# Rows that are put off, counted for four tiles at once: a top-p attention step on one Trainium2 core

## The chip, the cores and the metric

The kernel runs on one core of one Trainium2 chip. The metric is the device time of one execution in microseconds; the median of several executions is compared. A core has five engines, each with its own queue of instructions that it works off in order: TensorE (PE, with its weight loads PEld), VectorE (DVE), ScalarE (ACT), GpSimd (POOL) and SyncE (SP, which only issues DMAs here). They wait for each other, and for DMAs, through semaphores.

## The reference

Four layers of a graph network on 4096 nodes with 256 features and one 4096x4096 adjacency matrix. The layer that matters here is the second one, which runs two steps of this:

```python
def _top_p_attention(X, W1, W2, W3):
    q = X @ W1.T @ W2.T
    k = X @ W3.T
    logits = q @ k.T / TAU
    probs = jax.nn.softmax(logits, axis=-1)
    idx = jnp.argsort(-probs, axis=-1)
    sp = jnp.take_along_axis(probs, idx, axis=-1)
    cs = jnp.cumsum(sp, axis=-1)
    keep_sorted = cs - sp < TOP_P            # TOP_P = 0.9
    ...
    A = probs * mask
    return A / jnp.maximum(A.sum(-1, keepdims=True), 1e-12)

for n in range(STEPS):                       # STEPS = 2
    A = _top_p_attention(Xa, W1, W2, W3)
    Xf = R @ Xf
    Xa = A @ Xa
    Z = Z + Xf @ U1[n].T + Xa @ U2[n].T
```

R is the adjacency matrix with the identity added, rows normalised. The sum X + Z is layer-normalised, then the layer's residual is added and normalised again: two normalisations per row, each with one reciprocal square root.

## The kernel before

The 4096 rows are worked on as NT = 32 tiles of 128 rows (P = 128), the 4096 columns as NLC = 8 chunks of 512. In the profile, layer 0 lies at 0 to about 390 us, step 0 of the attention layer from there to about 1440 us, step 1 from about 1440 to 2690 us, the last two layers after that.

An iteration i of `run_step` has three tiles in work: logits of tile i + 2 (matmuls L414, copied by ACT), the selection for tile i + 1, and the mixing product of tile i (`acc_bank`, L761 and L769). The selection finds the threshold of each row from the largest entries: maxima by groups of eight (`cand`, L433), a scan of their sum, a threshold `t_thr`, then `match_replace` (L658) and four passes over the row of exponentials (L663). Rows for which this way is not sure to give the exact set are marked in a column `bad` (L564), 1.0 or 0.0 for each of the 128 rows. They are put off: their numbers go into a list in DRAM, `list_d`, and jobs (`put_off`, L897 and on) later take 128 of them at a time, compute them by an exact way and write them over the first result. Step 0 has one such job, step 1 has three (`LATER = (1, 3)`).

The list is made by `flag` (L582 to L607), once per tile. With `bad` as the moving operand PE multiplies by a matrix of ones (the tile's count, in every partition) and by a triangular matrix `before` (how many bad rows stand ahead of this one in the tile), L592 and L593; in the profile each is two passes. Three DVE operations follow: the new running count `sofar` (L595), `slot` (L599) and `slots` (L600), which is the place in the list for a bad row, and a spare place for all others. Then POOL scatters the tile's 128 row numbers to these places by an indirect DMA (L606). It is 64 scatters in all, each to the tensor `list_d` of its step. The scatters of a step have each to wait until the one before has landed, since they write one tensor.

The products of `flag`, of the queries (L394) and of the mixing (L822) take turns in the two halves of one PSUM bank, `mm_bank`.

An iteration's operations are hung on the eight chunks g = 0 to 7 in a fixed order:

```python
at(2, tops, cd, rounds)
at(2, pick, cd, rounds)
at(4, flag, cd)
```

`at(5, settle)` follows in step 1, where `match_replace` and L663 are. In step 0 the indirect gathers of the kept neighbours (`G`, L672, 512 in all) are hung on g = 4 to 7 and fill POOL's queue. A scheduler then orders instructions by priority for each engine, within what the program's dependences allow; each engine executes its own list in that order.

At the end of an iteration `after` makes the output of tile i: `mix` (h, L822 and L824) and two layer normalisations, whose reciprocal square roots are single operations on POOL (`rstd`, L199). DVE uses them at L848 (first normalisation, with the residual) and L204 (second).

A job starts at the end of the iterations that `starts` names: i = 30 in step 0 and i = 9, 20 and 30 in step 1. It starts with a DMA of 128 entries of the list on SP's queue (`to_l`, L888), a DVE operation on them (`from_l`, L890) and an indirect gather of the rows on POOL (`xf_new`, L812); its other stages run beside the next eight iterations. A job may start only when the scatters of all tiles up to i + 1 have been made.

Of the kernel before, what the change touches and what calls it, by code (L numbers as in the profile page):

```python
# [11 lines left out]
F32 = mybir.dt.float32  # L12
# [7 lines left out]
ALU = mybir.AluOpType  # L20
# [4 lines left out]
P = 128  # L25
# [15 lines left out]
LATER = (1, 3)  # L41
ROUNDS = 9
NG_LATER = 18
KEPT = 16
MATCHES_LATER = 3
MATCHES = 1
# [10 lines left out]
def gnn_stack(ctx, tc, x, adjt, adjn, w0, b0, w1, w2t, w3t, u1t, u2t, ln_g, ln_b, w2, b2, w3, b3, out):  # L57
# [3 lines left out]
    nc = tc.nc  # L61
    N = x.shape[0]
    NT = N // P
    LC = min(512, N)
    NLC = N // LC
# [20 lines left out]
    def half(bank):  # L86
        turns[bank] ^= 1
        return (mm_bank if bank == "mm" else acc_bank)[:, turns[bank], :]
# [268 lines left out]
    with tc.tile_pool(name="l1", bufs=1, reuse_waits="tile") as l1:  # L357
# [64 lines left out]
        def small(tag, w=1, dt=F32, bufs=2):  # L422
            if cur["late"]:
                return cur["lw"].tile([P, w], dt, tag=tag, name=f"{tag}_l", bufs=2 if w == 1 else 1)
            return work.tile([P, w], dt, tag=tag, name=tag, bufs=bufs)
# [108 lines left out]
        def pick(st, rounds):  # L534

            top, thr, base = st["top"], st["thr"], st["base"]
            W = 8 * rounds  # L540
            cs = small("cs", W + 1, bufs=1)
            if base is None:
                nc.vector.memset(cs[:, 0:1], 0.0)
                te = small("te", W + 1)
                nc.scalar.activation(te, top, AF.Exp, bias=st["m"], scale=1.0)
            else:
                nc.vector.tensor_copy(cs[:, 0:1], base)
                te = top
            nc.vector.memset(cs[:, W:], 3e38)
            nc.vector.tensor_tensor_scan(cs[:, 1:W], te[:, : W - 1], te[:, : W - 1], cs[:, 0:1], op0=ALU.add, op1=ALU.max)  # L550
            under, part = small("under", W, bufs=1), small("part", W, bufs=1)
            count = small("count")
            nc.vector.tensor_scalar(under, cs[:, :W], thr, 0.0, op0=ALU.is_lt, op1=ALU.add, accum_out=count)
            nc.vector.scalar_tensor_tensor(part, cs[:, 1:], thr, under, op0=ALU.is_ge, op1=ALU.mult)
            st["t"] = t = small("t_thr")
            nc.vector.scalar_tensor_tensor(part, part, 1.0, te[:, :W], op0=ALU.mult, op1=ALU.mult, accum_out=t)
            st["left"] = left = small("left")
            nc.vector.tensor_scalar(part, te[:, :W], t, 0.0, op0=ALU.is_ge, op1=ALU.add, accum_out=left)
            nc.vector.tensor_sub(left, left, count)
            st["bad"] = bad = small("bad")  # L560
            nc.vector.tensor_tensor(bad, te[:, W - 1 : W], te[:, W:], op=ALU.max)
            nc.vector.tensor_tensor(bad, bad, t, op=ALU.is_ge)
            most = 0.0 if sparse(st) else 8.0 * (MATCHES if base is None else MATCHES_LATER)
            nc.vector.scalar_tensor_tensor(bad, left, most, bad, op0=ALU.is_gt, op1=ALU.max)  # L564
            if sparse(st):

                same = small("same")
                for r in range(8, W, 8):
                    nc.vector.tensor_tensor(same, top[:, r - 1 : r], top[:, r : r + 1], op=ALU.is_equal)
                    nc.vector.tensor_tensor(bad, bad, same, op=ALU.max)  # L570
                st["w"] = w = small("w", W)
                kept = small("kept")
                nc.vector.scalar_tensor_tensor(w, te[:, :W], t, te[:, :W], op0=ALU.is_ge, op1=ALU.mult, accum_out=kept)
                whole(st, kept)
# [7 lines left out]
        def flag(st):  # L582


            pb = half("mm")
            later = st.get("later")
            if later is None:
                nc.tensor.matmul(pb[:1, 0:1], st["bad"], ones_col, start=True, stop=True)
                st["nb"] = small("nbad", 1, I32)[:1, :]
                nc.scalar.copy(st["nb"], pb[:1, :1])  # L590
                return
            nc.tensor.matmul(pb[:, 0:1], ones_sq, st["bad"], start=True, stop=True)  # L592
            nc.tensor.matmul(pb[:, 1:2], before, st["bad"], start=True, stop=True)  # L593
            sofar, slot = small("sofar"), small("slot")
            nc.vector.tensor_add(sofar, later["base"], pb[:, 0:1])  # L595

            i = st["tile"]
            at, rows_i = slots_of[cur["n"]][:, i : i + 1], ids[:, i : i + 1]
            nc.vector.scalar_tensor_tensor(slot, pb[:, 1:2], later["base"], spare, op0=ALU.add, op1=ALU.subtract)  # L599
            nc.vector.scalar_tensor_tensor(at, slot, st["bad"], spare, op0=ALU.mult, op1=ALU.add)  # L600
            later["base"] = sofar
            if i == NT - 1 and cur["n"] == 0:

                st["to"] = to = small("to_last", 1, I32, 1)
                nc.vector.scalar_tensor_tensor(to, st["bad"], float(P), rows_i, op0=ALU.mult, op1=ALU.add)
            nc.gpsimd.indirect_dma_start(  # L606
                out=list_d[cur["n"]], out_offset=bass.IndirectOffsetOnAxis(ap=at, axis=0), in_=rows_i, in_offset=None)  # L607

        def bit_by_bit(st):

# [333 lines left out]
        def run_step(n, es):  # L944

            later = {"base": spare0}
            tiles = {}
            last = []  # L950
            jobs = []
# [26 lines left out]
                cur["late"] = False  # L978
                return [[f] for f in after(n, job["st"])]

            starts = {min((k + 1) * NT // LATER[n] - 1, NT - 2): k for k in range(LATER[n])}
            for i in range(-2, NT):
                st = tiles.pop(i, None)
                cd = tiles.get(i + 1)
                nxt = None
                if i + 2 < NT:

                    nxt = {"tile": i + 2, "q": cur["qs"].pop(0), "e": logits_in(es[i % 2]), "later": later, "G": {}}
                    tiles[i + 2] = nxt
                if i + 1 == NT and n == 0:  # L990
                    for fs in last:
                        for f in fs:
                            f()
                    last = []
                    left_over(n, es[NT % 2], later)
                ops = {}

                def at(g, f, *args):
                    ops.setdefault(g, []).append(lambda: f(*args))

                for g, fs in zip((1, 2), last):
                    for f in fs:
                        at(g, f)
                if 0 < i + 2 < NT - 1:
                    turned = []
                    g = 1 if n else 6
                    at(g - 1, lambda i, turned: turned.append(transposed(cur["xa"][:, i + 3, :])), i, turned)
                    at(g, lambda turned: cur["qs"].append(query(None, turned[0])), turned)
                if cd is not None:
                    peak_groups(cd, NG_LATER if n else ngr)  # L1010
                    at(1, exp_rows, cd)
                for job in jobs:
                    at(1, advance, job)
                if cd is not None:
                    rounds = ROUNDS if n else KEPT // 8
                    at(2, tops, cd, rounds)
                    at(2, pick, cd, rounds)
                    at(4, flag, cd)
                    if n == 0:
                        for k in range(8):  # L1020
                            at(4 + k // 2, gather, cd, k)
                    else:
                        at(5, lambda cd: [None for _ in settle(cd)], cd)
                for job in jobs:
                    if n and i + 1 == NT:
                        at(4, advance, job)
                    at(6, advance, job)
                if i + 1 == NT and n == 0:
                    cur["next"] = load_halves(es[1 - NT % 2], xf_d, nc.sync)
                if i < 0:  # L1030
                    now = FIRST[n][i + 2]
                else:
                    now = [i + 2] if FIRST[n][1][-1] < i + 2 < NT else []
                pieces(n, st, nxt, ops, now)
                last = [[f] for f in after(n, st)] if st is not None else []
                if i in starts:
                    k = starts[i]
                    if len(jobs) > (i == NT - 2):
                        last = finish(jobs.pop(0), last)
                    e = es[NT % 2] if k + 1 == LATER[n] else es[2]  # L1040
                    jobs.append({"stages": put_off(n, k, e, later)})
                    if i < NT - 2:
                        advance(jobs[-1])
# [185 lines left out]
```

## Time and profile before

| | us |
|---|---|
| median of 3 runs | 3159.19 (3156.39 to 3160.6) |
| the profiled execution | 3226.1 |
| its span in the trace | 3224.4 |
| PE busy | 2945.7 (91%) |
| DVE busy | 2260.9 (70%) |
| ACT busy | 1729.6 (54%) |
| POOL busy | 778.7 (24%) |
| scatter L606, one, on POOL | 1.02 (64 of them) |

The profile comes from one execution with the profiler on, which took longer than the runs that are timed; durations below are of that execution. A line of the timeline reads: start in us from the span's start, duration in us, engine, line of the kernel, operation, output<-inputs, shape, count, and in brackets how long the engine stood idle before it and what ended that. SPq is the issue queue of SyncE. [...]

### The profile page before, as it was taken

Reading aid. Unit: us, or ns where it says so; the run is one execution under the profiler, and the core shown is the slowest. Engines: PE = TensorE matmul, PEld = TensorE weight load, DVE = VectorE, ACT = ScalarE, POOL = GpSimd, SP = SyncE. Lnnn points to the kernel's source line nnn. Section 1 sums busy time; section 2 is a strip of 40 time slices with the busy share of each in tenths; the row PEclk is TensorE's granted clock in tenths of the full one; section 3 lists DMA queues with packets and bytes.
Section 4 is the critical chain, followed back from the end, with each engine's and each line's share of the span. In section 5 each row is a group of like instructions: output and inputs, shape, how many; then the busy total and the mean of one; then the engine's idle time right before and its main releaser. Section 6 shows DMA issues by size and latency. Waiting matters only on the chain. (4 is left out here: it accounts for less than half of the span.)

```text
span 3224.4 us, 45413 instructions
## 1 busy us (share of the span) xinstructions
PE 2945.7 (91%) x14244; PEld 2313.2 (72%) x14244; DVE 2260.9 (70%) x7159; ACT 1729.6 (54%) x2883; POOL 778.7 (24%) x908
## 2 busy tenths in 40 slices
PE   7999888999989997779998999999999986999998
PEld 3788666777767775567777787778887654777886
DVE  4666667778777776447998898986999654444444
ACT  3555545556555554545554655555555434666664
POOL 1121256666666665100000000010000100000000
PEclk9999988999999998889999999999999997999999
DMA  9995467777777776241000011111111234333332
GB/s 169 157 178 121 82 96 121 140 140 138 139 134 138 134 135 135 88 122 38 24 24 23 27 37 32 32 35 33 38 34 29 85 108 143 107 108 97 107 107 79
DMA packets 247484, 299.44 MB, mean 93 GB/s; under 512 B 34464, under 2 KB 201312, under 8 KB 247232
## 3 DMA queue, kind: packets, MB, share of 16 engines
q0 software_dynamic: 46336, 104.28, 23.5%
q1 hardware_dynamic: 188656, 180.93, 18.7%
q10 hardware_dynamic: 12240, 11.23, 1.1%
q8 instruction: 115, 1.88, 0.3%
q14 instruction: 137, 1.12, 0.2%
HBM read 330.65 MB, written 66.32 MB: 123 GB/s over the span
## 5 line engine op out<-in xcount | busy, mean ns | idle before, releaser
L686 PE MATMUL acc_r<-xh,adjq 128*128 128x512 f32 x2048 | 619.3, 431 | 31.5 <-ACT adjq L683 17.1
L769 PE MATMUL acc_bank<-xa,at 128*128 128x256 f32 x2240 | 548.7, 385 | 26.8 <-ACT at L747 26.4
L672 POOL DMA_INDIRECT G<-x_d,cols x512 | 498.5, 974 | 296.1 <-PE acc_bank L761 143.3
L683 ACT CAST adjq<-adj 128x512 fp32r<-128x512 fp8e4 x512 | 316.4, 620 | 431.4 <-PE acc_r L686 237.2
L769 PEld LDWEIGHTS acc_bank<-xa,at 128*128 128x128 f32 x2240 | 408.3, 192 | 85.9 <-ACT at L747 38.1
L686 PEld LDWEIGHTS acc_r<-xh,adjq 128*128 128x128 f32 x2048 | 379.4, 191 | 125.8 <-ACT adjq L683 38.3
L433 DVE MAX8 cand<-e 128x8 f32<-128x228 f32 (+1 forms) x1088 | 387.3, 402 | 81.2 <-ACT e L415 44.8
L415 ACT COPY e<-lg 128x512 f32<-128x512 f32 x544 | 315.7, 586 | 209.2 <-PE lg L414 172.6
L199 POOL TENSOR_TENSOR rstd<-ve,mhalf 128x1 f32<-128x1 f32 x166 | 100.5, 606 | 1334.2 <-DVE ve L197 1274.0
L414 PE MATMUL lg<-kS,q 128*128 128x512 f32 x1088 | 391.9, 445 | 9.8 <-issue 5.5
L1109 ACT CAST a<-a 128x1024 fp32r<-128x1024 fp8e4 x256 | 268.4, 1050 | 167.0 <-PE acc L175 127.8
L761 PE MATMUL acc_bank<-G,dg 128*128 128x256 f32 x1024 | 291.8, 405 | 46.8 <-DMA G<-x_d,cols 15.1
L530 DVE FIND_INDEX8 cols<-top,e 128x8 uint32<-128x4096 f32 x64 | 282.8, 4419 | 0.0
L175 PE MATMUL acc<-xh,a 128*128 128x512 f32 x1024 | 262.1, 410 | 20.0 <-DMA x2i<-x_d 16.2
L761 PEld LDWEIGHTS acc_bank<-G,dg 128*128 128x128 f32 x1024 | 199.5, 200 | 104.5 <-issue 23.4
L175 PE MATMUL acc<-y0h,a 128*128 128x512 f32 x1024 | 249.8, 397 | 0.0
L175 PEld LDWEIGHTS acc<-xh,a 128*128 128x128 f32 x1024 | 193.3, 192 | 67.5 <-ACT xh L151 21.7
L175 PE MATMUL acc<-yh,a 128*128 128x512 f32 x1024 | 237.9, 394 | 0.0
L175 PEld LDWEIGHTS acc<-yh,a 128*128 128x128 f32 x1024 | 192.1, 188 | 43.8
L175 PEld LDWEIGHTS acc<-y0h,a 128*128 128x128 f32 x1024 | 187.9, 188 | 38.9 <-issue 0.6
L747 ACT COPY at<-at_ps 128x512 f32<-128x512 f32 x288 | 168.9, 588 | 82.4 <-PE at_ps L744 79.6
L414 PEld LDWEIGHTS lg<-kS,q 128*128 128x128 f32 x1088 | 182.3, 195 | 32.4 <-ACT e L415 11.1
(287 smaller groups left out, 4447.1 us busy)
## 6 DMA issues: line engine op xcount, KB each, us to landing
adj<-adj_d SPq DMA_DIRECT2D x256, 128.0 KB
a<-adj_d SPq DMA_DIRECT2D x256, 128.0 KB
a<-in_adjt POOLq DMA_DIRECT2D x64, 256.0 KB
adj_d<-a SPq DMA_DIRECT2D x64, 256.0 KB
adjn<-in_adjn POOLq DMA_DIRECT2D x64, 256.0 KB
x_d<-x SPq DMA_DIRECT2D x64, 128.0 KB
xf_d<-xf_new SPq DMA_DIRECT2D x64, 128.0 KB
G<-x_d,cols POOLq DMA_INDIRECT x512
```

Of the source, the lines that this page charges most:

```text
L175: nc.tensor.matmul(acc, a[:, j, :], halves(jt), start=(jt == 0), stop=(jt == NT - 1))
L414: nc.tensor.matmul(pl[:, :LC], q[k], kS[:, s], start=(k == 0), stop=(k == 1))
L415: nc.scalar.copy(l[:, s], pl[:, :LC])
L433: nc.vector.max(dst[:, 8 * g : 8 * g + 8], src[:, g * w : min((g + 1) * w, N)])
L530: nc.vector.max_index(st["at"][:, 8 * r : 8 * r + 8], t8, st["e"][:, :N])
L672: nc.gpsimd.indirect_dma_start(out=g, out_offset=None, in_=x1_d, in_offset=bass.IndirectOffsetOnAxis(ap=st["at"][:, k : k + 1], axis=0))
L683: nc.scalar.copy(a, cur["a8"][:, g % 2 * GP : (g % 2 + 1) * GP, :])
L686: nc.tensor.matmul(acc_r, a[:, j, :], xf[:, jt, :], start=(jt == 0), stop=False)
L747: nc.scalar.copy(at[:, :G, :], ps[:, :G, :])
L761: nc.tensor.matmul(acc_a, dg[:, k % 4, :], st["G"][k], start=(k == 0), stop=(k == KEPT - 1))
L769: nc.tensor.matmul(acc_a, ats[g][:, j, :], cur["xa"][:, jt, :], start=(jt == 0), stop=(jt == NT - 1))
L1109: nc.scalar.copy(a, a8)
```

## The change

- The `bad` columns of up to four tiles are collected in one tile of four columns (`bads`). After tiles 3, 7, ..., 27, and after tiles 30 (three columns) and 31 (one), they are counted at once: the same two products with up to four columns, a copy and a scan over the four counts for the running count, and three DVE operations on up to four columns for the slots.
- The scatters stay one per tile, 64 in all. In step 0 a queue gives one to each tile (`pend`), with the rest at the last tile; in step 1 all columns of a flush are scattered at the flush, one after the other.
- In step 1 `flag` is hung on the last chunk (g = 7) in place of g = 4, and the first of its products keeps its place in the program's order. In step 0 it stays on g = 4.
- The jobs' starts are put on the iterations after which the last counted tile is i + 1: in step 1 i = 10, 22 and 30 in place of 9, 20 and 30; in step 0 i = 30 as before.

```diff
+AT_ONCE = 4
...
-            st["bad"] = bad = small("bad")
+            later = st.get("later")
+            if later is None:
+                st["bad"] = bad = small("bad")
+            else:
+                if later["from"] is None:
+                    later["from"] = st["tile"]
+                    later["bads"] = work.tile([P, AT_ONCE], F32, tag="bads", name="bads", bufs=2)
+                c = st["tile"] - later["from"]
+                st["bad"] = bad = later["bads"][:, c : c + 1]
...
-            nc.tensor.matmul(pb[:, 0:1], ones_sq, st["bad"], start=True, stop=True)
-            nc.tensor.matmul(pb[:, 1:2], before, st["bad"], start=True, stop=True)
-            sofar, slot = small("sofar"), small("slot")
-            nc.vector.tensor_add(sofar, later["base"], pb[:, 0:1])
-
-            i = st["tile"]
-            at, rows_i = slots_of[cur["n"]][:, i : i + 1], ids[:, i : i + 1]
-            nc.vector.scalar_tensor_tensor(slot, pb[:, 1:2], later["base"], spare, op0=ALU.add, op1=ALU.subtract)
-            nc.vector.scalar_tensor_tensor(at, slot, st["bad"], spare, op0=ALU.mult, op1=ALU.add)
-            later["base"] = sofar
+            i, n = st["tile"], cur["n"]
...
-            nc.gpsimd.indirect_dma_start(
-                out=list_d[cur["n"]], out_offset=bass.IndirectOffsetOnAxis(ap=at, axis=0), in_=rows_i, in_offset=None)
+            if i % AT_ONCE == AT_ONCE - 1 or i >= NT - 2:
+                first, bads = later["from"], later["bads"]
+                w = i + 1 - first
+                later["from"] = None
+                pb = half("mm")
+                total = nc.tensor.matmul(pb[:, :w], ones_sq, bads[:, :w], start=True, stop=True)
+                if n:
+                    tc.keep_in_program_order(total)
+                nc.tensor.matmul(pb[:, AT_ONCE : AT_ONCE + w], before, bads[:, :w], start=True, stop=True)
+                sofar, slot = small("sofar", AT_ONCE + 1), small("slot", AT_ONCE)
+                nc.vector.tensor_copy(sofar[:, 0:1], later["base"])
+                nc.vector.tensor_tensor_scan(sofar[:, 1 : w + 1], pb[:, :w], bads[:, :w], sofar[:, 0:1], op0=ALU.add,
+                                             op1=ALU.max)
+                nc.vector.scalar_tensor_tensor(slot[:, :w], pb[:, AT_ONCE : AT_ONCE + w], spare, sofar[:, :w],
+                                               op0=ALU.subtract, op1=ALU.add)
+                nc.vector.tensor_mul(slot[:, :w], slot[:, :w], bads[:, :w])
+                nc.vector.tensor_scalar(slots_of[n][:, first : i + 1], slot[:, :w], spare, None, op0=ALU.add)
+                later["base"] = sofar[:, w : w + 1]
+                later["pend"] += range(first, i + 1)
+            for _ in range(len(later["pend"]) if n or i == NT - 1 else 1):
+                if later["pend"]:
+                    k = later["pend"].pop(0)
+                    nc.gpsimd.indirect_dma_start(
+                        out=list_d[n], out_offset=bass.IndirectOffsetOnAxis(ap=slots_of[n][:, k : k + 1], axis=0),
+                        in_=ids[:, k : k + 1], in_offset=None)
...
-            starts = {min((k + 1) * NT // LATER[n] - 1, NT - 2): k for k in range(LATER[n])}
+            starts = {}
+            for k in range(LATER[n]):
+                i = (k + 1) * NT // LATER[n] - 1
+                starts[min(i + (AT_ONCE - 2 - i) % AT_ONCE, NT - 2)] = k
...
-                    at(4, flag, cd)
+                    at(NLC - 1 if n else 4, flag, cd)
```

## The prediction

> **What bounds the kernel now.** I read the windows by stage first, then the timeline of one tile per phase, then the rows of the tensor `list_d` and the chain around a job's start. The profiled execution took 3226.1 us (span 3224.4), 2.1% above the median of 3159.19; the sums below are made in its time and carried over at the end. The columns of the windows are: stretch, its length, then busy time of PE, PEld, DVE, ACT and POOL, granted clock, DMA share, GB/s.
>
> ```profile
> 768.00:1264.00 496.00, 454.02 (x2456) 354.72 (x2456) 383.26 (x1125) 282.88 (x546) 322.60 (x339) 0.97 0.76 135
> 1503.00:1766.00 263.00, 242.96 (x1279) 203.92 (x1278) 239.00 (x835) 136.16 (x226) 20.33 (x27) 1.00 0.08 24
> 1806.00:2060.00 254.00, 240.92 (x1193) 197.48 (x1192) 235.03 (x790) 140.77 (x234) 15.55 (x21) 0.98 0.16 34
> 2214.00:2462.00 248.00, 237.36 (x1199) 195.77 (x1198) 235.84 (x789) 139.47 (x236) 15.57 (x21) 1.00 0.16 35
> ```
>
> Step 0 (first row) is bound by TensorE: 92% PE against 77% DVE. Step 1 without a job (second row) has PE and DVE both at 91 to 92%, in a period of 29.3 us per tile: a loop in which each waits for the other. Step 1 with a job running (the last two rows) has both at 93 to 96% over about 34 us; DVE's gaps are some 2 us per tile, so little is to be had there. GpSimd is nearly empty in step 1, but what DVE waits for stands in its queue:
>
> ```profile
> 1609.56 0.65 POOL L199 TENSOR_TENSOR rstd<-ve,mhalf 128x1 f32<-128x1 f32 x1 [23.74 <-DVE ve L197]
> 1610.92 0.48 DVE L848 SCALAR_TENSOR_TENSOR h<-h,rstd,x 128x256 f32<-128x256 f32 x1
> ...
> 1613.67 1.02 POOL L606 DMA_INDIRECT list_d<-ids,slots  x1 [3.46 <-DVE kept L578]
> 1614.72 0.58 POOL L199 TENSOR_TENSOR rstd<-ve,mhalf 128x1 f32<-128x1 f32 x1
> 1615.34 0.41 DVE L204 TENSOR_SCALAR h<-h,bn,rstd 128x256 f32<-128x256 f32 x1 [1.15 <-POOL rstd L199]
> ...
> 1620.10 0.14 DVE L466 TENSOR_SCALAR m<-m 128x1 f32<-128x1 f32 x1
> ```
>
> Every tile takes two `rstd` from POOL, and one scatter of 1.02 us ahead of the second already costs DVE 1.15 us. How long a scatter is under way shows where a job reads the list:
>
> ```profile
> 1759.69 1.02 POOL L606 DMA_INDIRECT list_d<-ids,slots  x1 [3.46 <-DVE kept L578]
> 1768.63 0.33 SPq L888 DMA_DIRECT2D to_l<-list_d  x1
> 1770.81 0.15 DVE L890 TENSOR_SCALAR from_l<-to_l 128x1 int32<-128x1 int32 x1 [6.36 <-DMA to_l<-list_d]
> ...
> 2143.39 1.02 POOL L606 DMA_INDIRECT list_d<-ids,slots  x1 [3.44 <-DMA x<-x1b_d]
> 2149.90 0.33 SPq L888 DMA_DIRECT2D to_l<-list_d  x1
> 2152.79 0.15 DVE L890 TENSOR_SCALAR from_l<-to_l 128x1 int32<-128x1 int32 x1 [4.83 <-DMA to_l<-list_d]
> ```
>
> The load waits for the scatter's landing alone and starts 8.94 and 6.51 us after the scatter. The trace's semaphore updates agree: of each scatter's 16, the last comes 8.9 and 6.5 us after its start, and over the 32 scatters of step 1 from 6.5 to 10.0 us, 8.4 in the mean. I call this L.
>
> **What the Trainium skill says.** "DMA: Bandwidth & Descriptors", section "Anatomy of one DMA — SWDGE (gpsimd) path": a DMA's fixed cost is about 2 us, mostly the write receipt, and waits on semaphores happen on the issuing engine. The trace agrees on the place, not the size: L is 8.4 us for 512 bytes, and I use L. The same page, "Why a DMA increments its semaphore by 16 and not by 1": only the sixteenth update means landed; that is how I read L. "Perfetto Trace Analysis", section "DMA Instruction — SWDGE (GPSIMD)": the profiler's end is the end of descriptor generation; so the row's 1.02 us hides the rest, as 8.94 beside it shows. "TensorEngine Tiling (Array Packing)", section "Instruction Overhead": a matmul with one column takes as long as one with 60; the trace has 250 ns for 128x1 and I price 128x4 the same.
>
> **The change part by part.** Savings first.
> (a) Step 0: 32 flags become 9. A flag takes 0.45 us of PE's queue (from 768.92 to the next `lg` weights at 769.37), and PE is the bound: 23 x 0.45 = -10 us. Five DVE operations replace 4 x 3; DVE has slack there.
> (b) Step 1, tiles without a job (10): PE gives back 0.55 us per flag (1611.34 to 1611.89) in three of four tiles, about -4.
> (c) Step 1 with jobs (some 20 tiles): PE waits for `bad` 37.2 us in 31 waits over the whole run; with the flag last, bad is long ready. But DVE is as full, so I count its share alone: 0.2 us of waiting and 0.33 us of operations per tile, minus a flush of about 0.9 us (five small operations of 0.14 to 0.22) every fourth: 20 x 0.53 - 5 x 0.9 = -6; bounds 0 and -20 (1 us per tile, if PE's wait counted in full up to DVE's gaps).
> Together -20 us.
>
> Now the costs. Each scatter to `list_d` waits for the landing of the one before (all write one tensor). In the kernel before they are 24 us or more apart, and this costs nothing. Afterwards, in step 1, four stand back to back on POOL, and the orders of the engines' instructions, as built, have each wait on its predecessor's DMA. So a flush holds POOL for 0.3 + 3L + 1.0 us = 26.5, and the next `rstd` ends 0.6 later: 27.1 us after `slots`. What stands behind is rstd, then a job's gathers; DVE waits for them in order, PE for DVE's `h`.
> (d) Tiles 3 and 7: `slots` stand two `MAX8` behind `m`, at m + 1.9. DVE reaches the first `h` that needs rstd at m + 20.1 (1610.92 less the m of the tile before, 1620.10 - 29.28 = 1590.8). rstd is there at m + 29.0: 8.9 us of stall; the 1.15 us of before goes. Taken +8 each: +16.
> (e) Tiles 15 and 27: in DVE's order slots come behind the four `e` operations L663 and sc (1914.9 in a tile of this kind), the h comes at 1925.15, 10.2 us later: 27.1 - 10.2 = 16.9 each: +34.
> (f) Tile 19: one rstd stands between third and fourth scatter. First h: 0.3 + 2L + 1.6 = 18.7 against 10: 9; the second another 3: +12.
> (g) Tile 11, job 0. to_l may start after the fourth landing, m + 1.9 + 0.3 + 4L = m + 35.8; the load took 2.2 us (1768.63 to 1770.81): m + 38. DVE reaches from_l right behind `match_replace`, at m + 15: a stall of 23 instead of 6.4: +17. rstd is inside it. SP waits at to_l too, with res, x and adj loads behind it; DVE stands longer than they need.
> (h) Tile 23, job 1: the same, from_l behind one L663 later, m + 17: 21 instead of 4.8: +16.
> (i) Tiles 30 and 31: three scatters, rstd 18.7 us after slots against about 15 us of work (estimate: 39 operations, four of them 1.28): +4. Job 2 waits for one scatter only, but its slots now stand behind the four L663: +4.
> (j) Step 0's end: the scatters of tiles 28 to 30 stand two gathers apart, so POOL waits some 6 us twice; POOL is busy 18 of 27.5 us per tile. That cover hides most: +3; uncovered +12.
> (k) Jobs 0 and 1 start one and two tiles later. All their instructions move, gathers on POOL and loads on SP included, over the same 8 iterations: +2, bounds 0 and +8.
> Costs 108. Against them, each stall leaves the other engines ahead, and their gaps in the following tile (some 1.5 us) close: seven times, -10. Net 108 - 10 - 20 = +78 us: 3304 in the profiled time, and as waits for landings do not shrink with the profiler off, 3159 + 78 = **3237 us**.
> Bounds of what before does not show: the pitch of scatters back to back is nowhere in it. At L = 7.5 and 9.3 the sum moves by 26 us per us of L (3 in each of the five flushes of (d) to (f), 4 at each of two job starts, 3 in (i)): -23 and +23. The scan's price is at most the row of the existing one (L550, 0.35 us): under 1 us in all.
>
> **The rivals.**
> *Partial (3185).* The pitch is that of the shortest landing, 6 us, and DVE gets part back. (d) +3 each, (e) 10 each, (f) 5, (g) and (h) 7 each, (i), (j) 11: 56, less 10 and 20: +26. For it: one landing took 6.49. Against: 26 of 32 took over 7.5.
> *Larger (3269).* After each flush PE and DVE restart empty, and PE pays a further 4 us (a job's start costs PE 7.2 us where DVE loses 6.4): seven times 4.5 on top: 78 + 32 = +110. Against: at job 1 PE lost 3.6 where DVE lost 4.8.
> *Not slower (3144).* If back-to-back scatters land as fast as their first semaphore update comes (2.3 us and more), 3 x 2.5 + 1.6 = 9 us is under the 10.2 and 18 us that DVE needs before rstd. Then only the savings remain, and to_l comes no later than now: -20 + 5 for the moved jobs = 3144. It decides from a pitch of about 3 us downwards. Against: 16 updates were needed each time to_l started.
> *No change (3159).* The spread between, a pitch near 4.5: loss and gain cancel.
>
> **How the numbers follow.** Likeliest 0.58, partial 0.18, larger 0.15, not slower 0.06, no change 0.03. The likeliest one's own range is 3212 to 3260; to leave out less than 2 in 10 it is widened to 3190 to 3268. A change of 0.2% (6.3 us) is about what a measurement of this kernel can tell from none: slower 0.91, same 0.03, faster 0.06.
>
> **What would show it.** Right: DVE's `h` L871 and L205 (the new lines of L848 and L204) with gaps of 8 to 17 us released by rstd at the flush tiles, scatters in step 1 some 8.4 us apart in fours, from_l waiting about 20 us for to_l in jobs 0 and 1, step 0 about 10 us shorter, layers 0, 2 and 3 unchanged. Wrong: scatters 1 us apart on POOL, or gaps at rstd under 3 us. If step 0 does not shorten, (a) is wrong; if the gaps are there and the time is not, the stalls replaced other waits that I took as work.

## The result and the profile after

The change makes the kernel slower: 3338.68 us (3325.61 to 3349.29) beside 3159.89 us (3152.88 to 3169.46) of the kernel before, 6 runs each; ratio 1.0562, 95% interval 1.0542 to 1.0582. That is +179 us where +78 was forecast.

One caution on lengths: beside the experiments below the kernel before took 3223 us, as in its profile (3226), while beside the changed kernel it took 3160, and the changed kernel's profile belongs to the latter. The profiler does not make this difference: the changed kernel's profiled execution, 3341.87 us, is one of its six. What makes it is open; in the two traces of the changed kernel, this one and e11, 72 of the 86 us between the spans lie ahead of the first `xa_new` of step 1. Lengths are therefore compared only within the set of the experiments, in which the changed kernel was profiled once more (e11); all other comparisons are ratios. At that set's speed, which is also that of the profile from which the prediction's sums are made, the change costs 197 us (e11).

The page of the changed kernel, parts 1 and 5:

```profile
PE 2935.3 (88%) x14060; PEld 2311.6 (69%) x14060; DVE 2245.2 (67%) x7057; ACT 1723.6 (52%) x2883; POOL 765.1 (23%) x908
...
L784 PE MATMUL acc_bank<-G,dg 128*128 128x256 f32 x1024 | 293.6, 406 | 133.2 <-DMA G<-x_d,cols 127.6
```

The same row of the kernel before:

```profile
L761 PE MATMUL acc_bank<-G,dg 128*128 128x256 f32 x1024 | 291.8, 405 | 46.8 <-DMA G<-x_d,cols 15.1
```

All engines are busy a little less than before (PE 2945.7, DVE 2260.9, POOL 778.7), and the span grew: most of the time went into waiting (what else there is comes with e11). The row shown is the mixing product of step 0; PE stood 133.2 us idle ahead of it, 127.6 of them for gathers. In the kernel before it was 46.8, of which 15.1 for gathers.

What was idle ahead of the scatters and the loads of the list, and who waited for them (rows of `list_d`, changed kernel; us, times):

```profile
L628 POOL DMA_INDIRECT list_d<-ids,slots x64: 955/1002/1085, 479.9 to 2629.7; - x64
...
  DMA list_d<-ids,slots: 285.2, 45
...
  POOL list_d L628: 292.0, 46
  DVE from_l L913: 47.8, 3
...
DMA to landing us min/median/max: 7.1/7.9/9.1
```

POOL waited 285.2 us in 45 places for a scatter's landing before it could issue the next scatter; in the kernel before this entry does not exist. `from_l` waited 47.8 us at three job starts, against 17.1.

Step 0, POOL and PE at one flush (timeline of the changed kernel):

```profile
609.22 0.99 POOL L628 DMA_INDIRECT list_d<-ids,slots  x1 [6.37 <-DMA list_d<-ids,slots]
...
611.11 0.99 POOL L695 DMA_INDIRECT G<-x_d,cols  x1 [0.30 <-PE mm_bank L853]
612.41 0.95 POOL L695 DMA_INDIRECT G<-x_d,cols  x1 [0.30 <-PE nef_ps L719]
618.05 1.00 POOL L628 DMA_INDIRECT list_d<-ids,slots  x1 [4.69 <-DMA list_d<-ids,slots]
619.36 0.95 POOL L695 DMA_INDIRECT G<-x_d,cols  x1 [0.31 <-issue]
...
623.53 2.08 PE L784 MATMUL acc_bank<-G,dg 128*128 128x256 f32 x4 [10.96 <-DMA G<-x_d,cols]
```

The program gives one scatter to a tile, but here they stand two gathers apart: scatter, two gathers, wait for the landing, scatter. The gathers that PE needs come behind, and PE stands for 10.96 us. It is so at every flush of step 0 but the first (there the gathers between them are none, none and four), not only at its end. A flush is the counting of up to four tiles, with the scatters that follow from it.

Step 1, tile 7, and the start of job 0 (timeline of the changed kernel):

```profile
1734.05 0.96 POOL L628 DMA_INDIRECT list_d<-ids,slots  x1 [6.25 <-DMA list_d<-ids,slots]
1735.03 0.57 POOL L200 TENSOR_TENSOR rstd<-ve,mhalf 128x1 f32<-128x1 f32 x1
1735.64 0.48 DVE L871 SCALAR_TENSOR_TENSOR h<-h,rstd,x 128x256 f32<-128x256 f32 x1 [8.67 <-POOL rstd L200]
...
1843.57 0.97 POOL L628 DMA_INDIRECT list_d<-ids,slots  x1 [9.06 <-DMA list_d<-ids,slots]
1851.30 0.96 POOL L628 DMA_INDIRECT list_d<-ids,slots  x1 [6.76 <-DMA list_d<-ids,slots]
1858.91 0.96 POOL L628 DMA_INDIRECT list_d<-ids,slots  x1 [6.66 <-DMA list_d<-ids,slots]
1866.06 0.33 SPq L911 DMA_DIRECT2D to_l<-list_d  x1
1868.96 0.15 DVE L913 TENSOR_SCALAR from_l<-to_l 128x1 int32<-128x1 int32 x1 [22.35 <-DMA to_l<-list_d]
```

The fourth scatter, rstd and DVE's `h` follow each other without a gap: DVE's 8.67 us are the scatters' landings. At the job's start the last three scatters stand 7.6 to 7.7 us apart, and the load of the list comes 7.15 us after the last one.

### The profile page after: what moved, and what is told of

The parts are those of the page before. It is cut to its first block, busy times and chain, and to the rows that moved or that the text cites. A ratio compares the mean times of both kernels' runs of the same rounds, so it can differ in the third digit from the quotient of the medians.

```text
span 3340.1 us, 44921 instructions
## 1 busy us (share of the span) xinstructions
PE 2935.3 (88%) x14060; PEld 2311.6 (69%) x14060; DVE 2245.2 (67%) x7057; ACT 1723.6 (52%) x2883; POOL 765.1 (23%) x908
## 5 line engine op out<-in xcount | busy, mean ns | idle before, releaser
L709 PE MATMUL acc_r<-xh,adjq 128*128 128x512 f32 x2048 | 641.6, 442 | 37.9 <-ACT adjq L706 27.2
L792 PEld LDWEIGHTS acc_bank<-xa,at 128*128 128x128 f32 x2240 | 416.2, 195 | 118.3 <-ACT at L770 67.2
L709 PEld LDWEIGHTS acc_r<-xh,adjq 128*128 128x128 f32 x2048 | 391.9, 196 | 128.9 <-ACT adjq L706 43.7
L784 PE MATMUL acc_bank<-G,dg 128*128 128x256 f32 x1024 | 293.6, 406 | 133.2 <-DMA G<-x_d,cols 127.6
```

The source lines that it names most:

```text
L709: nc.tensor.matmul(acc_r, a[:, j, :], xf[:, jt, :], start=(jt == 0), stop=False)
L784: nc.tensor.matmul(acc_a, dg[:, k % 4, :], st["G"][k], start=(k == 0), stop=(k == KEPT - 1))
L792: nc.tensor.matmul(acc_a, ats[g][:, j, :], cur["xa"][:, jt, :], start=(jt == 0), stop=(jt == NT - 1))
```

## The experiments

Ratios are to the kernel before, run beside each. "Step 0" and "step 1" lengths are from the traces: up to the first and from the first to the last `xa_new` of step 1 (kernel before: 1502.8 and 1154.6 us). Kernels with the same step 0 differed by up to 16 us in the first length (1494.7 to 1510.5), so single digits of it mean nothing; kernels with the same step 1 differed by up to 7.5 us in the second (e3, e7, e8: 1153.5 to 1161.0).

**e1, e2: the change in one step alone.** In e1 step 1, in e2 step 0 keeps the `flag` of before (`flag_one`), its place and, in e1, the job starts of before. `SINGLE` names that step.

```diff
-                    at(NLC - 1 if n else 4, flag, cd)
+                    at(4 if n in SINGLE else NLC - 1 if n else 4, flag_one if n in SINGLE else flag, cd)
```

> Counting for four tiles at once in step 0 alone; step 1 as in the kernel before (one flag per tile at g = 4, job starts 9, 20, 30). Theory A (each scatter to the list waits for the landing of the one before, and in step 0 four of them stand two gathers apart at every fourth tile, so POOL's gathers and with them PE stop for some 18 us): about 3160 + 85 = 3245 us, the part of the loss that the step-1 windows do not account for. Rival B (step 0 gains its 10 us as predicted, and all of the loss is step 1's): about 3150.

> The change in step 1 alone; step 0 as in the kernel before. Theory A: about 3160 + 93 = 3253 us, the growth of step 1 between the two traces. Rival B: about 3330, nearly all of the loss. If 3200 or less, the two steps' losses do not add.

e1: ratio 1.0301 (1.0273 to 1.0330), +97 us; step 0 took 1603.5 us, +101. e2: 1.0316 (1.0275 to 1.0358), +102 us; step 1 took 1259.3, +105. Rival B is out: step 0 does not gain, it loses as much as step 1. The sum of both, 6.2%, is the whole within its interval (e11).

**e3: four lists.** Each column of a flush goes to a list of its own; a job takes the least entry of the four.

```diff
-                        out=list_d[n], out_offset=...
+                        out=list_d[n][k % 4], out_offset=...
...
-            nc.sync.dma_start(to, list_d[n][slots, :])
+            parts = small("to_all", 4, I32)
+            for c in range(4):
+                nc.sync.dma_start(parts[:, c : c + 1], list_d[n][c][slots, :])
+            nc.vector.tensor_reduce(to, parts, axis=AX.X, op=ALU.min)
```

> The change as it is, but each of a flush's four columns has a list of its own in DRAM (slots unchanged; a job loads the same slots of all four lists and takes the least entry, since the three others hold a blank there), so that no scatter waits for the one just before it. Theory A: all stalls at flushes and most of the job starts' stalls go, the savings stay: 3100 to 3150, below before. Rival C (the losses come from the moved flag, the later job starts or the instructions' new order, not from the landings): still over 3250.

Ratio 1.0102 (1.0070 to 1.0134). Five sixths of the loss is gone, so the chain of landings is the cause of that part and rival C falls; but the expectation was missed too, for the kernel is not faster than before. Step 1 took 1153.5 us (-1), step 0 still 1534.1 (+31). What holds step 0 is another wait for a landing (timeline of e3, POOL):

```profile
611.36 0.97 POOL L628 DMA_INDIRECT list_d<-ids,slots  x1 [0.30 <-issue]
...
619.60 0.98 POOL L695 DMA_INDIRECT G<-x_d,cols  x1 [0.30 <-remote]
626.56 0.94 POOL L695 DMA_INDIRECT G<-x_d,cols  x1 [5.98 <-DMA list_d<-ids,slots]
```

A gather, which has nothing to do with the list, waited 5.98 us for a scatter given out some 15 us before. The trace's semaphores show why: POOL's DMAs take the eight semaphores 111 to 118 in turn, each behind the landing of the DMA eight before it. This gather counts on semaphore 116, as the flush's third scatter (at 610.09) did, and POOL waits ahead of it for 116 and 117, the semaphores of the third and the fourth. Between tiles 4 and 27 of step 0 such a wait is there seven times, 30.4 us.

**e4: step 0's scatters kept apart.** The change, with each scatter of step 0 held in the program's order.

```diff
-                    nc.gpsimd.indirect_dma_start(
+                    put = nc.gpsimd.indirect_dma_start(
...
+                    if n in (0,):
+                        tc.keep_in_program_order(put)
```

> The change as it is, but in step 0 each scatter is held behind what POOL was given before it in the program, so that the four of a flush are spread over four tiles, 16 gathers or so apart. Theory A: step 0's loss goes but for its last tiles: 3240 to 3260. Rival C: 3320 or more, since counts, waits and positions on PE and DVE are unchanged.

Ratio 1.0337 (1.0304 to 1.0369), the same as e2 within its interval, and step 0 took 1503.4 us: the whole of step 0's loss is gone. Behind a flush's first, second, third and fourth scatter stand mostly 4, 16, 16 and 28 gathers now, in place of 2, 2, 2 and 58. On the other engines nothing changed its place: from tile 2 to tile 30 the traces of e4 and e11 show one and the same order on DVE and on ACT, and on PE but for six records that one of them lacks. (The expectations' times in e1 to e4 start from the 3160 us of the other set; only their distances count.)

**e5, e6: the moves alone.** The kernel before with the flag at g = 7, its first product pinned (e5), and with the job starts 10, 22, 30 (e6). The edit of e5 (`flag_one` is the `flag` of before, `SINGLE` both steps):

```diff
-            nc.tensor.matmul(pb[:, 0:1], ones_sq, st["bad"], start=True, stop=True)
+            total = nc.tensor.matmul(pb[:, 0:1], ones_sq, st["bad"], start=True, stop=True)
+            if cur["n"]:
+                tc.keep_in_program_order(total)
...
-                    at(4, flag, cd)
+                    at(NLC - 1 if n else 4 if n in SINGLE else NLC - 1 if n else 4, flag_one if n in SINGLE else flag, cd)
```

> The kernel before with one part of the change: in step 1 the flag, still one per tile with its own scatter, stands at the last chunk and its first product keeps its place. If the wait of PE for bad (37 us in all) was worth what the prediction took, step 1 gets about 6 us shorter per 20 tiles with a job and 4 in the others: ratio 0.997. Rival E: slots now come behind the four passes L663, so the job starts wait longer and eat this: 1.000 or above.

> The kernel before with one part of the change: jobs 0 and 1 start at i = 10 and 22 in place of 9 and 20; flags as before. The prediction took +2 us with bounds 0 and +8: ratio 1.0006, up to 1.0025. Rival: if the starts are what makes step 1 slow, 1.01 or more.

e5: 0.9989 (0.9973 to 1.0004), not told from no change; in its trace step 1 is 5.8 us shorter, which is within the spread of such lengths. e6: 1.0025 (1.0011 to 1.0039), +8 us: the upper bound of what was forecast for the later starts.

**e7, e8: step 1 alone with four lists; both steps with four lists and step 0 kept apart.**

> The change in step 1 alone, with four lists in place of one (no scatter waits for the one just before it). Theory A: the 3 percent that step 1 alone cost goes entirely: 0.998 to 1.002. Rival C (order and positions cost it): 1.02 or more.

> The change with four lists in both steps, and in step 0 each scatter held behind what POOL was given before it. In the run with four lists step 0 was still 31 us longer: seven times a gather waited for the landing of a scatter (30 us), as if it needed the semaphore of the DMA eight before it. Theory D: with the scatters a tile apart this goes too, and step 0 shows what the counting for four tiles saves by itself: 23 flags of 0.45 us, ratio 0.996 to 0.999. If step 0 stays 20 us or more longer, the remaining loss of step 0 has another cause.

e7: 1.0010 (0.9997 to 1.0023). Step 1's 3.2% is gone. What the counting saves is not seen either; DVE still waits 14.06 and 8.74 us for the list at the starts of jobs 0 and 1, where it was 6.36 and 4.83, and starting later alone costs 8 us (e6). e8: 1.0017 (1.0000 to 1.0035); step 0 took 1503.5 us, so the rest of e3's step 0 goes when the scatters are spread as in e4. The 23 flags saved do not show as time there: the products with `bad` fell from 12.8 to 3.4 us of PE between tiles 4 and 27, but PE's idle time in that stretch was 57.4 us against 49.3, and e8's ratio is no lower than e7's. The saving that theory D expected was not seen.

**e9: two lists**, to see whether the loss goes with the time under way or with the number of scatters that wait.

> The change with two lists in place of one: a flush's third scatter waits for its first, the fourth for its second. Theory A, with 8.4 us per landing: POOL is held 0.3 + 8.4 + 1.3 + 1.0 = 11 us at a flush of step 1 in place of 26.5; rstd then comes before DVE needs it at tiles 3 and 7 (18 us after slots) and about 1 us late at the others (10.2); in step 0, with two gathers between, a scatter waits some 1 us in place of 5 to 6. Only the job starts stay later: ratio 1.010 to 1.020, close to the run with four lists. Rival: the loss goes with the number of scatters that wait at all (half of them): about 1.035.

Ratio 1.0081 (1.0057 to 1.0104). Some of the scatters still wait (19 times, 88.6 us, in place of 45 and 309.8 in e11), and six sevenths of the loss is gone; tiles 3 and 7 show no stall (28.6 us): this fits that what counts is whether POOL comes free before DVE or PE needs what stands behind it. The forecast of 1.010 to 1.020 was slightly high, the rival's 1.035 is out. Two lists do no worse than the four of e3 (the intervals overlap), and the landings show a reason: two scatters in flight land 7.4 to 10.4 us after their start in step 1, but of the four that e3 starts 1.3 us apart the third and fourth take 12.1 to 14.3 us, where the first two take 7.5 to 10.1 (scatters with all 16 updates in the traces).

**e10: a version of the parts that pay.** Step 0 as before, step 1 with four lists, and the tile ahead of a job's start counted alone.

```diff
+ENDS = (3, 7, 9, 10, 14, 18, 20, 21, 25, 29, 30, 31)
+ALONE = (10, 21, 31)
...
-            if i % AT_ONCE == AT_ONCE - 1 or i >= NT - 2:
+            if i in ENDS:
...
-                    at(NLC - 1 if n else 4, flag, cd)
+                    at(4 if n in SINGLE or i + 1 in ALONE else NLC - 1, flag_one if n in SINGLE else flag, cd)
```

> A version put together from the runs: step 0 as in the kernel before; in step 1 counting at the last chunk for up to four tiles at once with four lists, but flushes after tiles 3, 7, 9, 14, 18, 20, 25, 29 and 30, and the last tile ahead of each job's start (10, 21, 31) counted alone at g = 4; job starts as in the kernel before. The tiles without a start took 28.84 and 33.4 us in the batched runs against 29.28 and 33.9 before: some 8 x 0.44 + 14 x 0.5 = 10 us, less about 2 for the three loads more at each start: ratio 0.997. If the starts still cost as much as with four lists, 1.000 or above.

3197.44 us beside 3223.18, ratio 0.9925 (0.9900 to 0.9950): faster than both kernels. In its trace step 1 took 1138.1 us, 16.5 less than before, where some 8 were expected: the job starts got shorter too (36.3 us for the tile of job 0 in place of 40.4). The rest of the gain lies in step 0, whose code is that of before: 1491.9 us, just under the spread of such traces, so it is not credited to the edit.

**e11: the changed kernel beside the same runs of the kernel before.**

> The changed kernel itself once more, beside the same runs of the kernel before as the other two, for a trace of it on a chip on which the kernel before takes 3222 us. If the two steps' losses simply add: 1.0301 + 0.0316 = 1.062; less if a stall of step 0 also pays for something in step 1.

Ratio 1.0611 (1.0568 to 1.0655), as the two parts add. Step 0 took 1598.2 us (+95), step 1 1260.5 (+106). The waits of POOL ahead of the scatters in this trace:

```profile
  DMA list_d<-ids,slots: 309.8, 45
```

Waiting is not all of the loss. Tiles 4 to 27 of step 0, in the kernel before and in e11 (columns as in the prediction):

```profile
559.80:1194.80 635.00, 585.69 (x3198) 456.93 (x3197) 500.24 (x1474) 367.96 (x714) 415.51 (x438) 0.98 0.76 136
564.30:1287.80 723.50, 605.15 (x3131) 462.17 (x3129) 493.20 (x1435) 367.39 (x714) 413.78 (x439) 0.92 0.71 120
```

Of the 88.5 us more, 69 are idle time of PE (118.4 in place of 49.3). The other 19 are operations of PE, which took longer, though they are fewer: the mean granted clock of the stretch is 0.92 in place of 0.98. In e4, where the waits are gone, PE is busy 581.3 us there and the clock is 0.98. That the clock falls because PE stands was not tried by itself.

## Why the prediction was wrong

The direction and the mechanism were right: slower, by scatters that wait for each other's landing while POOL's queue stands. The size was not: less than half of the loss was forecast, because the mechanism was applied to one of two steps.

- **Step 0 is the step that failed: (a), with (j).** The prediction took -10 us from 23 flags there and allowed 3 to 12 us for "the scatters of tiles 28 to 30", two gathers apart. For the flushes ahead of them it put nothing, as if each tile had one scatter, as the program gives them. In the built order the four scatters of every flush but the first stand two gathers apart. Measured: +95 to +101 us (e11, e1) in place of -7. POOL's slack was priced once ("hides most: +3") and not for these flushes: by the prediction's own figures POOL has some 9.5 us to spare in a tile, and in e11 it waits 18 to 22 us for landings at each of these flushes of four. The gathers behind come late, and PE stands for them. e4 shows that the scatters' places alone do this. That PE's operations would take longer as well, 19 us in e11, stands nowhere in the prediction.
- **Step 1 was sized nearly right.** Forecast: +85 (108 of costs less 3 for step 0's end, less 10 for gaps that close and 10 for the savings of (b) and (c)). Measured: +105 and +106 in e2 and e11. The prediction's signs for it came true: gaps at `h` behind rstd, scatters 8.4 us apart, `from_l` waiting some 20 us. So did its sign that (a) is wrong: step 0 did not shorten. The stalls of DVE in e11, taken from its gaps, against the working:

| | forecast stall, us | e11 |
|---|---|---|
| tiles 3, 7 (d) | 8.9 | 8.50, 10.30 |
| tiles 15, 27 (e) | 16.9 | 14.22, 15.31 |
| tile 19 (f) | 9 + 3 | 11.22 + 7.06 |
| job 0 (g) | 23 | 24.30 |
| job 1 (h) | 21 | 21.33 |
| tile 30 (i) | 4 | 9.11 |
| job 2 (i) | 5.93 + 4 | 5.65 |

  The pitch of scatters back to back in step 1 lay between 6.7 and 10.5 us in e11, 8.4 in the mean; L = 8.4 from the updates of the kernel before was a sound price for an operation that its trace nowhere shows.
- **The -10 us for gaps that close behind a stall** is not supported: the pure tiles after a flush took 28.8 us like all others, so nothing was given back. With it gone, (k) 6 us more (e6), and the table's differences (together +5), step 1's sum comes to 85 + 10 + 6 + 5 = 106 us, against the 105 and 106 measured. That it fits to the microsecond is luck, for such lengths differ by up to 7.5 us.
- **(b) and (c):** tiles without a job took 28.84 us in place of 29.28, 0.44 each (forecast 0.41); e5's step 1 was 5.8 us shorter, which is not told from no change. The 37.2 us in 31 waits were a misreading: they add 15.6 us in 15 waits of PE and 21.6 us in 16 waits of its weight loads, which run beside each other. PE's wait for `bad` was thus about half of what (c) started from; that (c) counted on DVE's share alone kept this out of the sum.
- **L.** The Trainium skill's fixed cost of about 2 us for a DMA ("DMA: Bandwidth & Descriptors", section "Anatomy of one DMA — SWDGE (gpsimd) path") would have led to the rival "not slower"; the semaphore updates of this case's trace, 8.4 us, were the better source, as taken. (The first of a scatter's 16 updates comes 2.0 us and more after its start, not 2.3 as the rival has it, which changes nothing there.)

The partial rival was off in the wrong direction; the larger one put 32 us more into the restart of PE and DVE in step 1, for which the sum above leaves no room, and nothing into step 0.

## What to carry to other kernels

Before counting what a batch saves, look at where the built order puts every DMA it emits, in each stage, and not only in one sample: here four scatters that became ready together were issued close together, though the loop gives one to a tile. As built here, indirect DMAs that write one tensor follow each other at the time of a landing (8.4 us), not of an issue (1.3 us), and what stands behind them in POOL's queue waits along. Tensors of their own (e3, e7, e9) or more work between them (e4) took this away; four tensors did no better than two. And set a stall against the slack of the engine that has it, in every stage.

## What was not expected of the hardware

- A scatter of 128 single words took 6.9 to 11.3 us to land in the changed kernel's trace, from its start to the last of its 16 semaphore updates, with 1.0 us of it on the issuing engine's row; a gather of 128 rows of 1 KB landed in 4.4 us (median of `G`).
- Of four scatters in flight the third and fourth took 12.1 to 14.3 us (e3, step 1), with two in flight 7.4 to 10.4 (e9).
- A gather can wait for scatters that it does not depend on, through a semaphore used again eight DMAs later: 5.98 us in the case shown of e3. More semaphores were not tried; with the scatters spread (e8) one such wait of 0.3 us is left in step 0.
- With PE's waits in step 0 the mean granted clock fell from 0.98 to 0.92 between tiles 4 and 27, and PE's operations took 19 us longer (e11).
